# A recurrence on one Trainium2 core: 16 columns of half B's z product go ahead of A2, and the x products of a block start 17 steps ahead instead of 16

## The chip, the cores and the metric

The kernel runs on one core of one Trainium2 chip. The metric is the device time of one execution in microseconds (us). TensorE multiplies matrices (PE in the profile, its weight loads PEld), VectorE (DVE) and ScalarE (ACT) read its results from PSUM, GpSimd (POOL) works on SBUF alone, and SyncE (SP) issues the DMAs.

## The reference

A gated recurrence over 512 time steps, with a batch of 8 and 512 units, all in float32; its input is added to its output:

```python
def step(h, x_t):
    fused = sigmoid(concatenate([x_t, h], -1) @ w_W + w_b)
    hidden_state, output_state = split(fused, 2, -1)
    memory_state = x_t @ wx_W + wx_b + hidden_state * (h @ wh_W + wh_b)
    h_new = output_state * h + (1.0 - output_state) * tanh(memory_state)
    return (h_new, h_new)
_, hs = scan(step, cond_1024, swapaxes(x, 0, 1))
return x + swapaxes(hs, 0, 1)
```

In the kernel's names, r is `hidden_state` and z is `output_state`. What depends on h must be computed step by step; what depends on x alone can be computed ahead.

## The kernel before, in words

**The recurrence.** The 512 units are cut into four chunks of 128. Chunks 0 and 1 are half A, chunks 2 and 3 are half B. The state h lies in `hT` with the units of a chunk on the partitions, and a ring of eight buffers holds it, one for each of eight steps. Four steps form a group, and all products of a group go into one set of three PSUM banks: `A` (256 columns: 64 of half B's h product, then half A's h product, z and r), `D` (128 columns: half B's z, then its r) and `H` (64 columns: the rest of half B's h product). There are two sets, for groups in turn.

Each step multiplies the new state by the recurrent weights in the order of the table `ORDER`: "A0" is bank A with chunk 0, and so on. A0 and A1 are 256 columns wide, A2 and A3 are 192 (the last of bank A's columns), D0 to D3 are 128, H2 and H3 are 64. Each entry is four matmuls, one for each 32 output partitions. In the trace each matmul counts twice, with a weight load ahead of each.

VectorE and ScalarE then make the new state (`turn_r`, `turn_h`, `turn_z`, `memory`, `update`): VectorE transposes half A's columns of bank A (`tr<-A`, `md1A<-A`, `tz<-A`), ScalarE takes the sigmoids, VectorE's scan forms the argument of tanh (`m`), ScalarE takes the tanh, and another scan forms the new state of half A, chunk by chunk. Half B follows from `md1B<-A`, `tr<-D`, `sz<-D` and `md1B<-H`. A0 and A1 need half A's state alone, A2, A3 and D2, D3, H2, H3 need half B's.

**The x side.** x is cut into blocks of 16 steps. For each block, the x part of all gates is computed by a nested scheme of seven products in each of seven (`products`), 49 units of 96 columns, three units in a step and four in one step of 16 (`deal`). They run behind H in TensorE's order. GpSimd forms the sums of x that the scheme needs (`x_sum`, `inner_x`). VectorE drains finished products from PSUM (`drain`, line 429: 384 or 288 columns), DMAs on SP's queue move parts of them between partitions (lines 431 and 433, `ff<-tt` and `ff<-ff`), GpSimd adds them up (`result`, line 448), and the sums end in `xs`. From there VectorE's `turn_x` (line 317) and ScalarE's `spread` (line 312) put the x part into the next group's buffers and banks, as the table `AHEAD` says for each of the last three steps of a group. The first blocks get their x part by plain passes, dealt over the first steps (`PLAIN` lists the steps with four passes instead of three).

`LEAD` is the number of steps by which a block's products begin ahead of the block. The steps of `drain`, of GpSimd's sums and of `result` are counted from it. The order of the work on each engine is the order of this program text; nothing reorders it but TensorE, which loads weights ahead of the running matmul.

Of the kernel before, what the change touches and what calls it, by code (L numbers as in the profile page):

```python
# [23 lines left out]
LAST = 4  # L24
SYNC = mybir.DependencyInfo(mybir.DependencyClass.Sync, mybir.DependencyReason.DATA)

ORDER = "A0 A1 A2 A3 D0 D1 D2 D3 H2 H3"

FIRST = "A0 A1 x A2 x x A3 H0 H1 H2 H3 x D0 D1 D2 D3"

# [22 lines left out]

PIECE = (((0, 384), (384, 672)), ((960, 1344), (672, 960)))

LEAD = 16

AHEAD = (
    (((), ""), ((0, 1), "AD"), ((2, 3), "H")),
    (((0,), "A"), ((1, 2), "D"), ((3,), "H")),  # L60
    (((0,), "A"), ((1,), "D"), ((2, 3), "H")),
    (((0,), "A"), ((1,), "D"), ((2, 3), "H")),
)

PLAIN = (5, 10, 15)

COLS = slice(64, 448)

# [6 lines left out]
def tile_cond_rnn_residual(  # L75
# [88 lines left out]
    wd = const.tile([P, NQ, NQ, 128], F32, name="wd")  # L164
# [51 lines left out]
    def mm(out_, lhsT, rhs, start=False):  # L216
        nc.tensor.matmul(  # L217
            out_, lhsT, rhs, start=start, stop=False, skip_group_check=True
        )
# [7 lines left out]
    def bank_of(g):  # L227

        return {2: whole[1]["H"], 3: whole[1]["A"], 4: whole[1]["D"]}.get(g, xps[g % 2])
# [70 lines left out]
    def keep(g):  # L300

        nc.scalar.copy(xs[g % GS][:, SC], bank_of(g)[:, COLS])
# [5 lines left out]
    def spread(g, names):  # L308

        for n in names:  # L310
            skip = 64 if n == "A" and not g else 0
            nc.scalar.copy(banks[g % 2][n][:, skip:], source(g, XP[n].start + skip, XP[n].stop))
# [59 lines left out]
    def x_sums(c):  # L372
        jobs = [(x_sum, c, n) for n in range(4)]
        return jobs + [(inner_x, c, n, p) for n in range(4) for p in (0, 2, 3)]
# [75 lines left out]
    def take(it, n=None):  # L450
        while n is None or n > 0:
            if next(it, it) is it:
                return
            n = None if n is None else n - 1
# [5 lines left out]
    def deal(it, n):  # L460

        while n > 0 and next(it, it) is None:
            n -= it.send(n)
# [28 lines left out]
    def at_step(i, *todo):  # L492
        jobs.setdefault(i, []).extend(todo)
# [10 lines left out]
    for c in range(2, NCH):  # L504
        w0 = TC * c - LEAD
        sums = x_sums(c)
        for n, q in enumerate(sums):
            late_one = n == len(sums) - 1
            at_step(w0 - 10 + n // 2 if c == 2 else w0 if late_one else w0 - 12 + (n + 1) // 2, q)
        unit = 0  # L510
        for q, order in zip(STAGES, ORDERS):
            for name in order:
                unit += PASS[name][2] // BL
                if name in (order[1], order[3]):
                    w = min((unit - 1) // 3, TC - 1)
                    drains.setdefault(w0 + w, []).append((q, PASS[name][0]))
        for e, w, jobs_ in ((0, 12, ((0, 3), (2, 4), (1,), (5, 6))), (1, 17, ((0, 3), (1, 2), (4, 5), (6,)))):
            for m, todo in enumerate(jobs_):
                at_step(w0 + w + m, *[(result, e, n) for n in todo])

    pool_done = {}
    for i in range(T):
        g, s = divmod(i, GS)
        c, t = divmod(i, TC)
        ps = banks[g % 2]
        if c > 0 and t in (1, 4, 7, 10):
            e, k = divmod(t // 3, 2)
# [4 lines left out]
        k_ = 0  # L532
        for n in (ORDER if i else FIRST).split():
            if n == "x":
                take(first[1], 1)
                if k_ == 0:
                    keep(2)
                k_ += 1
                continue
            bank, k = n[0], int(n[1])  # L540
            hs = hT[k // 2][i % NH][:, :, k % 2, 2]
            to, w_ = {
                "A": (ps["A"], wa) if k < 2 else (ps["A"][:, 64:], wa[:, :, :, 64:]),
                "D": (ps["D"], wd),
                "H": (ps["H"], wa[:, :, :, :64]),
            }[bank]
            if bank == "A" and i == 0:
                to, w_ = xps[0][:, :HALF], wa[:, :, :, 64:]
            for j in range(NQ):
                mm(to[32 * j : 32 * j + 32, :], hs, w_[:, k, j])  # L550
        if i == 0:
            take(first[1])
        elif i <= PLAIN[-1]:
            take(first[4], 3 + (i in PLAIN))
        else:
            deal(later, 4 if (i + LEAD) % TC == TC - 1 else 3)

# [138 lines left out]
        elif i > 3 and 0 < s and g + 1 < NG:  # L696
# [1 line left out]
            for e in es:  # L698
                turn_x(g + 1, e)
            spread(g + 1, names)  # L700
        if i in PLAIN:
            keep(4 + i // 5)
        if i == 6:
            seed(7)
        for w in late.get(i, ()):
# [107 lines left out]
```

## Time and profile before

| | |
|---|---|
| Time, median of 3 runs | 1630.92 us (1630.65 to 1631.48) |
| The profiled execution, its own time | 1628.26 us |
| Its span, first to last instruction | 1626.5 us |
| Busy: PE, PEld, DVE, ACT, POOL | 1616.7, 1308.8, 1413.1, 1024.2, 541.3 us |
| Granted TensorE clock | 1.0 throughout |
| DMA | 62.04 MB, 38 GB/s over the span |

The span holds 512 steps of some 3.1 us each. A row of the timeline gives the start in us, how long the row lasts, engine, line, operation, output and inputs, shape, how many equal instructions were merged, and in brackets the idle time before it and what ended it. A row that merges several matmuls shows the shape of the first: a row of bank A with x32 holds the 256-column products and the 192-column ones. A matmul's record reaches to the modelled end of its pass through the array, so records overlap, and the busy share of PE says less than the distance from one block's start to the next one's.

### The profile page before, as it was taken

Reading aid. Unit: us, or ns where it says so; the run is one execution under the profiler, and the core shown is the slowest. Engines: PE = TensorE matmul, PEld = TensorE weight load, DVE = VectorE, ACT = ScalarE, POOL = GpSimd, SP = SyncE. Lnnn points to the kernel's source line nnn. Section 1 sums busy time; section 2 is a strip of 40 time slices with the busy share of each in tenths; the row PEclk is TensorE's granted clock in tenths of the full one; section 3 lists DMA queues with packets and bytes.
Section 4 is the critical chain, followed back from the end, with each engine's and each line's share of the span. In section 5 each row is a group of like instructions: output and inputs, shape, how many; then the busy total and the mean of one; then the engine's idle time right before and its main releaser. Section 6 shows DMA issues by size and latency. Waiting matters only on the chain.

```text
span 1626.5 us, 120027 instructions
## 1 busy us (share of the span) xinstructions
PE 1616.7 (99%) x49211; PEld 1308.8 (80%) x49211; DVE 1413.1 (87%) x11757; ACT 1024.2 (63%) x6033; POOL 541.3 (33%) x1443
## 2 busy tenths in 40 slices
PE   9999999999999999999999999999999999999998
PEld 6888888888888888888888888888888888888876
DVE  8988888888888888888888888888888888888887
ACT  4666666666666666666666666666666666666665
POOL 2323333333333333333333333333333333333321
PEclk9999999999999999999999999999999999999999
DMA  4011111111111111111111111111111111111110
GB/s 192 12 34 34 31 39 38 38 35 30 36 41 41 31 31 35 42 38 33 33 33 39 38 38 35 29 37 41 41 31 31 35 42 38 33 34 28 32 35 10
DMA packets 66217, 62.04 MB, mean 38 GB/s; under 512 B 9856, under 2 KB 64000, under 8 KB 65664
## 3 DMA queue, kind: packets, MB, share of 16 engines
q1 hardware_dynamic: 65664, 54.35, 12.7%
q8 instruction: 385, 6.31, 1.7%
q14 instruction: 168, 1.38, 0.3%
HBM read 14.96 MB, written 8.39 MB: 14 GB/s over the span
## 4 chain that ended last, share of the span: by engine, by line
PE 98%; DVE 2%; issue 0%; ACT 0%
PE A L217 49%; PE D L217 27%; PE xp L217 16%; PE H L217 7%; DVE tr L575 0%; DVE m L563 0%; DVE md1B L634 0%; DVE hT L563 0%; DVE md1A L590 0%; DVE tz L575 0%; DVE zeros L183 0%; DVE hd0B L627 0%; DVE md1B L590 0%; DVE idle L598 0%; ACT hT L283 0%
## 5 line engine op out<-in xcount | busy, mean ns | idle before, releaser
L217 PE MATMUL A<-wa,hT 128*32 128x256 f32 x16352 | 877.7, 355 | 4.3 <-DVE hT L563 4.3
L217 PEld LDWEIGHTS A<-wa,hT 128*32 128x32 f32 x16352 | 497.9, 123 | 260.9 <-DVE hT L563 135.2
L217 PE MATMUL D<-wd,hT 128*32 128x128 f32 x16384 | 541.0, 273 | 0.0
L217 PEld LDWEIGHTS D<-wd,hT 128*32 128x32 f32 x16384 | 480.6, 122 | 21.6 <-DMA wd<-in_wd_dram 0.4
L729 POOL TENSOR_TENSOR ot<-xin,hT 128x32 f32<-128x32 f32 x503 | 135.2, 269 | 1040.9 <-DVE hT L563 960.2
L283 ACT ACTIVATE md0A<-tr 128x16 f32<-128x16 f32 x512 | 112.9, 220 | 384.0 <-DVE tr L575 383.9
L283 ACT ACTIVATE hT<-m 128x8 f32<-128x8 f32 x2048 | 324.1, 207 | 48.0 <-DVE m L563 2.4
L575 DVE STREAM_TRANSPOSE tr<-A 128x64 f32<-128x64 f32 x511 | 127.7, 250 | 198.0 <-PE A L217 197.1
L283 ACT ACTIVATE hT<-hT 128x16 f32<-128x16 f32 x1024 | 232.1, 227 | 92.0 <-DVE hT L563 85.4
L217 PE MATMUL H<-wa,hT 128*32 128x64 f32 x8208 | 208.3, 219 | 0.0
L283 ACT ACTIVATE md0B<-tr 128x8 f32<-128x8 f32 x1024 | 160.0, 206 | 42.5 <-DVE tr L575 1.2
L217 PEld LDWEIGHTS H<-wa,hT 128*32 128x32 f32 x8208 | 185.8, 122 | 0.0
L563 DVE TENSOR_TENSOR_SCAN hT<-hd0B,hT 128x24 f32<-128x24 f32 x1024 | 171.7, 208 | 1.1 <-DVE hT L563 1.1
L563 DVE TENSOR_TENSOR_SCAN hT<-hd0A,hT 128x24 f32<-128x24 f32 x1024 | 172.2, 168 | 0.0
L563 DVE TENSOR_TENSOR_SCAN m<-md0B,md1B 128x24 f32<-128x24 f32 x1024 | 154.4, 192 | 0.4 <-issue 0.4
L627 DVE STREAM_TRANSPOSE hd0B<-sz 128x32 f32<-128x32 f32 x1024 | 148.6, 190 | 0.0
L563 DVE TENSOR_TENSOR_SCAN m<-md0A,md1A 128x16 f32<-128x16 f32 x1024 | 143.6, 182 | 5.5
L217 PE MATMUL xp<-ti,si 128*32 128x192 f32 (+1 forms) x3120 | 146.7, 295 | 0.0
L448 POOL TENSOR_TENSOR xs<-ff 128x192 f32<-128x192 f32 x240 | 139.8, 599 | 0.0
L634 DVE STREAM_TRANSPOSE md1B<-A 128x64 f32<-128x64 f32 x511 | 129.9, 254 | 0.0
L283 ACT ACTIVATE hd0A<-tz 128x16 f32<-128x16 f32 x512 | 116.6, 228 | 20.9
L590 DVE STREAM_TRANSPOSE md1B<-H 128x64 f32<-128x64 f32 x512 | 128.1, 250 | 0.0
(110 smaller groups left out, 1860.3 us busy)
## 6 DMA issues: line engine op xcount, KB each, us to landing
ff<-tt SPq DMA_DIRECT2D x120, 96.0 KB, 2.1
ff<-tt SPq DMA_DIRECT2D x120, 72.0 KB, 2.0
out_dram<-ot SPq DMA_DIRECT2D x128, 64.0 KB, 1.8
xin<-in_x_dram SPq DMA_DIRECT2D x112, 64.0 KB, 2.2
ff<-ff SPq DMA_DIRECT2D x60, 96.0 KB, 3.0
ff<-ff SPq DMA_DIRECT2D x60, 72.0 KB, 2.2
wx<-in_wx_dram SPq DMA_DIRECT2D x4, 768.0 KB, 7.3
wa<-in_wa_dram SPq DMA_DIRECT2D x4, 512.0 KB, 11.1
```

The source lines that it names most:

```text
L217: nc.tensor.matmul(out_, lhsT, rhs, start=start, stop=False, skip_group_check=True)
L283: inst = nc.scalar.activation(out_, in_, func, **kw).ins
L448: nc.gpsimd.tensor_tensor(to, a, b, ALU.add)
L563: return nc.vector.tensor_tensor_scan(*[t_[:, :, c_].rearrange("p n c s -> p (n c s)") for t_ in (out_, d0, d1)], 0.0, ALU.mult, ALU.add,).ins
L575: inst = nc.vector.transpose(t_.rearrange("p c n -> p (c n)"), raw[n][hf]).ins
L590: inst = nc.vector.transpose(md1[hf][g % 2][:, :, :, hf].rearrange("p n c -> p c n"), raw["h"][hf]).ins
L627: nc.vector.transpose(hd0[1][i % 2][:, :, q, 2], sz[:, 32 * q : 32 * q + 32]).ins
L634: nc.vector.transpose(md1[1][g % 2][:, :, :, 0].rearrange("p n c -> p c n"), ps["A"][:, :HU])
L729: pool_done[i + 1] = nc.gpsimd.tensor_tensor(ot[:, t], x_of(c, slice(0, NQ), t, 1), hTs[(i + 1) % NH][:, :, :, B * s1 : B * s1 + B, 2].rea ...
```

## The change

The table `ORDER` gets two new kinds of entry. "F0" is the first 16 columns (`AHEAD_D`) of bank D with chunk 0, placed between A1 and A2; "L0" is the other 112 columns, where D0 stood. `LEAD` becomes 17; the steps of GpSimd's jobs are given one more, so that they stay where they were, while the products and their drains go one step earlier. `AHEAD` deals `turn_x` and `spread` differently, and `PLAIN` and the new `DONE` deal the 48 plain passes over 14 steps instead of 15.

```diff
-ORDER = "A0 A1 A2 A3 D0 D1 D2 D3 H2 H3"
+ORDER = "A0 A1 F0 A2 A3 L0 D1 D2 D3 H2 H3"
+
+AHEAD_D = 16
...
-LEAD = 16
+LEAD = 17
 
 AHEAD = (
-    (((), ""), ((0, 1), "AD"), ((2, 3), "H")),
+    (((), ""), ((0,), "AD"), ((1, 2, 3), "H")),
+    (((0,), "A"), ((1,), "D"), ((2, 3), "H")),
+    (((0,), "A"), ((1, 2, 3), "D"), ((), "H")),
     (((0,), "A"), ((1, 2), "D"), ((3,), "H")),
-    (((0,), "A"), ((1,), "D"), ((2, 3), "H")),
-    (((0,), "A"), ((1,), "D"), ((2, 3), "H")),
 )
 
-PLAIN = (5, 10, 15)
+PLAIN = (5, 6, 7, 8, 9, 14)
+
+DONE = (5, 9, 14)
...
-            at_step(w0 - 10 + n // 2 if c == 2 else w0 if late_one else w0 - 12 + (n + 1) // 2, q)
+            at_step(w0 - 9 + n // 2 if c == 2 else w0 + 1 if late_one else w0 - 11 + (n + 1) // 2, q)
...
-        for e, w, jobs_ in ((0, 12, ((0, 3), (2, 4), (1,), (5, 6))), (1, 17, ((0, 3), (1, 2), (4, 5), (6,)))):
+        for e, w, jobs_ in ((0, 13, ((0, 3), (2, 4), (1,), (5, 6))), (1, 18, ((0, 3), (1, 2), (4, 5), (6,)))):
...
                 "D": (ps["D"], wd),
+                "F": (ps["D"][:, :AHEAD_D], wd[:, :, :, :AHEAD_D]),
+                "L": (ps["D"][:, AHEAD_D:], wd[:, :, :, AHEAD_D:]),
                 "H": (ps["H"], wa[:, :, :, :64]),
...
-        if i in PLAIN:
-            keep(4 + i // 5)
+        if i in DONE:
+            keep(5 + DONE.index(i))
```

TensorE, one step of a later block, before: the state's buffer is `hT5`, and the rows behind H are x products.

```order
L217 MATMUL A1_172<-wa_79,hT5_95 32x256 x8
L217 MATMUL A1_172<-wa_79,hT5_95 32x192 x8
L217 MATMUL D1_173<-wd_86,hT5_95 32x128 x16
L217 MATMUL H1_174<-wa_79,hT5_95 32x64 x8
L217 MATMUL xp1_176<-ti_150,si0_153 32x192 x4
L217 MATMUL xp1_176<-ti_150,si0_153 32x96 x4
```

The same step in the changed kernel:

```order
L221 MATMUL A1_172<-wa_79,hT5_95 32x256 x8
L221 MATMUL D1_173<-wd_86,hT5_95 32x16 x4
L221 MATMUL A1_172<-wa_79,hT5_95 32x192 x8
L221 MATMUL D1_173<-wd_86,hT5_95 32x112 x4
L221 MATMUL D1_173<-wd_86,hT5_95 32x128 x12
L221 MATMUL H1_174<-wa_79,hT5_95 32x64 x8
L221 MATMUL xp1_176<-ti_150,so0_151 32x192 x4
L221 MATMUL xp1_176<-ti_150,so0_151 32x96 x4
```

Four matmuls of 16 columns now stand between the 256-column and the 192-column products of bank A, the first four of D have 112 columns, and the x products behind H are those that stood one step later.

VectorE, the end of step 107 (its number stands in `m1_107` and `sz_107`), before: the drain is the row of line 429.

```order
L563 SCALAR_TENSOR_TENSOR m1_107_10358<-md0B0_100,md1B0_104 128x24 x2
L627 STREAM_TRANSPOSE hd0B1_109<-sz_107_10376 128x32 x2
L630 MEMSET idle_148 128x1
L563 SCALAR_TENSOR_TENSOR hT4_94<-hd0B1_109,hT3_93 128x24 x2
L429 TENSOR_TENSOR tt_162<-xp1_176,ee2_159 128x288
L317 STREAM_TRANSPOSE md1B1_105<-xs3_166 128x32 x2
L708 MEMSET idle_148 128x1 x2
L575 STREAM_TRANSPOSE tr0_108_10455<-A1_172 128x64
```

The end of the same step in the changed kernel, where the drain is the row of line 433:

```order
L569 SCALAR_TENSOR_TENSOR m1_107_10798<-md0B0_100,md1B0_104 128x24 x2
L633 STREAM_TRANSPOSE hd0B1_109<-sz_107_10816 128x32 x2
L636 MEMSET idle_148 128x1
L569 SCALAR_TENSOR_TENSOR hT4_94<-hd0B1_109,hT3_93 128x24 x2
L433 TENSOR_TENSOR ff1_161<-xp0_175,ee1_158 128x384
L321 STREAM_TRANSPOSE md1B1_105<-xs3_166 128x32
L714 MEMSET idle_148 128x1 x2
L581 STREAM_TRANSPOSE tr0_108_10897<-A1_172 128x64
```

The drain into `tt`, whose DMAs GpSimd's jobs of step 108 read, stood at the end of step 107 and stands one step earlier now; the drain that stood in step 108 takes its place, and of the two transposes of `xs` one remains here. GpSimd's rows are the same in both kernels, in the same order.

## The prediction

> **What bounds the kernel now.** I read the page's busy shares and chain first, then the timeline of one step in the middle, then a step near the end that has no x products, then the single blocks of TensorE.
>
> ```profile
> PE 1616.7 (99%) x49211; PEld 1308.8 (80%) x49211; DVE 1413.1 (87%) x11757; ACT 1024.2 (63%) x6033; POOL 541.3 (33%) x1443
> ...
> PE 98%; DVE 2%; issue 0%; ACT 0%
> ```
>
> Read alone, this says that TensorE sets the time and that any column moved into an idle moment is a gain. The step shows something else. These are TensorE's products in two steps of the middle, and then its weight loads:
>
> ```profile
> 800.76 1.71 PE L217 MATMUL A<-wa,hT 128*32 128x256 f32 x32
> 802.29 1.06 PE L217 MATMUL D<-wd,hT 128*32 128x128 f32 x32
> 803.16 0.41 PE L217 MATMUL H<-wa,hT 128*32 128x64 f32 x16
> 803.39 0.35 PE L217 MATMUL xp<-wx,so 128*32 128x96 f32 x8
> 803.55 0.51 PE L217 MATMUL xp<-ti,si 128*32 128x192 f32 x8
> 803.88 1.72 PE L217 MATMUL A<-wa,hT 128*32 128x256 f32 x32
> 805.41 1.06 PE L217 MATMUL D<-wd,hT 128*32 128x128 f32 x32
> ```
>
> ```profile
> 803.81 0.64 PEld L217 LDWEIGHTS A<-wa,hT 128*32 128x32 f32 x16
> 804.72 0.51 PEld L217 LDWEIGHTS A<-wa,hT 128*32 128x32 f32 x16 [0.26 <-DVE hT L563]
> 805.25 0.96 PEld L217 LDWEIGHTS D<-wd,hT 128*32 128x32 f32 x32
> ```
>
> A step takes 3.12 us (800.76 to 803.88). Each chunk of h makes two blocks in the trace, and a block is four products that start together, one for each 32 output partitions. So D is 8 blocks of 128 columns in 0.87 us (802.29 to 803.16), 0.109 each, and H is 4 blocks of 64 columns in 0.23, 0.057 each: some 0.82 ns a column. By that rate a block of 256 columns takes 0.216 and one of 192 takes 0.162, and the step's products add up to 4 x 0.216 + 4 x 0.162 + 0.87 + 0.23 + 0.49 (xp, 803.39 to 803.88) = 3.10 us. TensorE is nearly full, but 0.02 us is missing. It is lost ahead of A2: the loads for A2 wait for half B's state until 804.72, as the row says.
>
> Whether TensorE or the recurrence sets 3.12 us is told by the last steps, where no x products are left. Loads first, then products:
>
> ```profile
> 1601.11 0.61 PEld L217 LDWEIGHTS A<-wa,hT 128*32 128x32 f32 x16 [0.39 <-DVE hT L563]
> 1602.01 0.51 PEld L217 LDWEIGHTS A<-wa,hT 128*32 128x32 f32 x16 [0.29 <-DVE hT L563]
> ...
> 1604.22 0.62 PEld L217 LDWEIGHTS A<-wa,hT 128*32 128x32 f32 x16 [0.39 <-DVE hT L563]
> ```
>
> ```profile
> 1601.11 1.78 PE L217 MATMUL A<-wa,hT 128*32 128x256 f32 x32 [0.24 <-DVE hT L563]
> 1602.70 1.06 PE L217 MATMUL D<-wd,hT 128*32 128x128 f32 x32
> ```
>
> There TensorE has 0.49 us less to do and idles, and the step still takes 3.11 us (1601.11 to 1604.22). So the loop sets the time: half B's state, A2 and A3, the transposes and scans on VectorE, the new state. VectorE releases half A's state and half B's 0.90 to 0.91 us apart in both places (1601.11 and 1602.01; 803.81 and 804.72), and A0 and A1 must fit between them.
>
> **The change part by part.** *The 16 columns.* Four matmuls are added to each of 511 steps (the first step has its own order), which is two blocks of 16 columns between A1 and A2; D's first two blocks shrink to 112 columns. What is given back, 2 x 16 x 0.82 ns = 0.027 us, lies behind A3, outside the loop, and only adds to TensorE's slack: I count nothing for it, and where TensorE itself is the bound I subtract it. What can be hidden is the room ahead of A2. For it I need the time from a load that was waited for to its product; the rows are a place where A0's loads came late, the first block's and the second block's, then the duration of that first block's products, the loads', and the usual one:
>
> ```profile
> 365.40 0.14 PEld L217 LDWEIGHTS A<-wa,hT 128*32 128x32 f32 x4 [0.44 <-DVE hT L563]
> ...
> 365.44 0.15 PEld L217 LDWEIGHTS A<-wa,hT 128*32 128x32 f32 x4
> ```
>
> ```profile
> L217 PEld LDWEIGHTS A<-wa,hT x8: 121/127/134, 365.4 to 365.5; 128*32 128x32 f32 x8
> L217 PE MATMUL A<-wa,hT x4: 418/418/418, 365.4 to 365.4; 128*32 128x256 f32 x4
> ...
> L217 PE MATMUL A<-wa,hT 128*32 128x256 f32 x4912 | 321.3, 379 | 0.0
> ```
>
> A product whose load has just been issued is recorded 418 ns long where 379 is usual, so it begins about 0.04 us after its load, and the next block's loads go out 0.03 to 0.04 us after the first block's. The room follows. In the middle step A0 could begin at 803.81 + 0.04 = 803.85, and TensorE reaches it at 803.88; A1 ends at 803.88 + 4 x 0.216 = 804.74, and A2 begins at 804.72 + 0.04 = 804.76. The room is 0.03 + 0.02. In the late step A1 ends at 1601.11 + 0.04 + 0.864 = 1602.014 and A2 begins at 1602.05: 0.036. I take 0.04 us.
>
> What the two blocks occupy is not in the trace, where no block is narrower than H's 64 columns. Bound from below by the rate: H's 0.057 less 48 columns of 0.82 ns is 0.018, twice 0.036. Bound from above by the loads: a block's weights are loaded while the block ahead of it runs, one block ahead and no further (D's first loads go out at 805.25 and D starts at 805.41, 0.16 later, which is A3's last block), and a 16-column block is over before the next load is done. The first block's weights are there in time, under A1's last block. The second block's loads go out when the first block starts; A2's loads can go out only when the second block has taken its weights, 0.035 later (the spacing of the two load rows), and A2 begins 0.04 after that: 0.075 us, and at most 2 x 0.04 = 0.08 if the loads do not overlap at all. I take 0.075, because a run of loads that nothing hides is just what the rows at 365.40 show. That is 0.035 more than the room. Nothing hides it: A2 is late by 0.035, so is everything on VectorE behind it, and half A's state of the next step with it. 511 x 0.035 = 17.9 us. The new blocks wait besides for ScalarE's read of D (sz) of the step before, done long since, so I count nothing for that wait.
>
> In one step of each chunk four units of x products are dealt instead of three, and there TensorE is the bound. The row before and after such a step:
>
> ```profile
> 871.24 0.25 DVE L575 STREAM_TRANSPOSE tr<-A 128x64 f32<-128x64 f32 x1 [0.26 <-PE A L217]
> ...
> 874.50 0.25 DVE L575 STREAM_TRANSPOSE tr<-A 128x64 f32<-128x64 f32 x1 [0.30 <-PE A L217]
> ```
>
> It takes 3.26 us. There the blocks cost 0.075 - 0.027 = 0.048, which is 0.013 over what I counted: 30 x 0.013 = 0.4 us.
>
> *Seventeen steps ahead.* The sums of the x products (drains, VectorE) and the DMAs behind them go one step earlier; GpSimd's jobs stay in their absolute steps, so a DMA has a step more to land. This is what a late one costs. The rows are GpSimd's and VectorE's at such a place, VectorE's scans in an ordinary step, and the waits:
>
> ```profile
> 364.10 1.18 POOL L448 TENSOR_TENSOR ff<-ff 128x192 f32<-128x192 f32 x2 [0.95 <-DMA ff<-tt]
> ...
> 364.20 0.64 DVE L563 TENSOR_TENSOR_SCAN m<-md0A,md1A 128x16 f32<-128x16 f32 x2
> ...
> 803.08 0.28 DVE L563 TENSOR_TENSOR_SCAN m<-md0A,md1A 128x16 f32<-128x16 f32 x2
> ```
>
> ```profile
> POOL ot L729 <- DMA ff<-ff: 5.6, 3, 2.1
> POOL ff L448 <- DMA ff<-tt: 4.3, 7, 1.2
> ```
>
> GpSimd's sum, released late, runs beside the scans of the loop, and they take 0.64 instead of 0.28 us. There are 10 such waits, each of at most 2.1 us and so shorter than the step that is won. Between nothing and 10 x 0.36 I take 0.2 each, since a wait may end clear of the scans: 2.0 us gained. On SP's queue a drain's DMA now passes one load of x or one store, each under a step long; nobody is close to those. VectorE's drains and turn_x are dealt so that no step gets more than a wide drain with one transpose or a narrow one with two, which is no more than before; the 0.40 us that VectorE waits for A in an ordinary step (802.54, below) stays its cover. At the start six steps instead of three have a fourth pass, for the same 48 passes: between 0 and 3 x 0.14 us, I take 0.2.
>
> *Sum.* 17.9 + 0.4 - 2.0 + 0.2 = 16.5 us. The profiled execution took 1628.26 (its span 1626.5 and 1.8 around it), so 1644.8; the median of the three timed runs is 2.66 above it, so the forecast is 1647 us, slower by 1.0%.
>
> **Rivals.** *Hidden.* If a 16-column block costs only its columns, the two fill 0.036 us of a room of 0.04, and the loop keeps its length. What is left is the gain at the DMAs: 1630.9 - 2.0 + 0.2 = 1629 us. For it speaks that the H blocks, half as wide as D's, show no cost beyond their columns; against it that H's 0.057 still covers a load of 0.04, and 0.018 does not. It decides below 0.04 us for the pair.
>
> *Issue alone.* Four loads last 0.14 us together and 0.121 each, so they go out 0.0065 apart, 0.027 for four. If loads pipeline and only that issue is left, the pair takes 0.054 and overruns by 0.014: 511 x 0.014 = 7.2, less 1.8, 1636 us. Against it speaks the spacing of 0.03 to 0.04 between the two load rows, where nothing but loads went on.
>
> The Trainium skill, "TensorE: Matmul & The Clock Gate", section "LDWEIGHTS (loading the stationary operand)", puts a load at its columns over 1.2 GHz, an estimate of 27 ns for 32 columns. By that page the result would be this rival's; no run here has shown such a block yet, and the load rows are nearer to 35 ns.
>
> *D is the real limit.* VectorE's transposes of A and of D, against the ends of those products (800.76 + 1.71 = 802.47; 802.29 + 1.06 = 803.35):
>
> ```profile
> 802.54 0.25 DVE L575 STREAM_TRANSPOSE tr<-A 128x64 f32<-128x64 f32 x1 [0.40 <-PE A L217]
> ...
> 803.27 0.25 DVE L634 STREAM_TRANSPOSE md1B<-A 128x64 f32<-128x64 f32 x1
> 803.42 0.24 DVE L575 STREAM_TRANSPOSE tr<-D 128x64 f32<-128x64 f32 x1
> ```
>
> ```profile
> 363.41 1.06 PE L217 MATMUL D<-wd,hT 128*32 128x128 f32 x32
> ...
> 364.77 0.24 DVE L634 STREAM_TRANSPOSE md1B<-A 128x64 f32<-128x64 f32 x1
> 364.92 0.20 DVE L575 STREAM_TRANSPOSE tr<-D 128x64 f32<-128x64 f32 x1
> ```
>
> Both transposes start 0.07 us after the end of what they read, and tr<-A certainly waited. If D is late too, taking 0.027 us out of it shortens every step: with the blocks hidden, 1629 - 511 x 0.027 = 1615 us. Against it: 0.15 us lie between md1B and tr<-D there, and just as many where D had been done for 0.45 us (364.47 against 364.92). VectorE's own pace sets that start.
>
> **How the numbers follow.** Forecast 0.62, hidden 0.18, issue alone 0.13, D 0.05, something else 0.02. The forecast's own range is 1642 to 1650, from 0.065 to 0.08 us for the pair; a miss of the DMA gain lies within it at 1649. The whole range reaches down to the hidden case and takes in issue alone: 1628 to 1653. A measurement can tell about 0.2%, 3.3 us, from no change. Slower by more: the forecast and nearly all of issue alone, 0.75. Within: most of the hidden case, 0.18. Faster by more: D and the best of the hidden case, 0.07.
>
> **What would show it.** In the new trace the loads for A2 should follow the first 16-column block by some 0.035 us instead of waiting for half B's state; A2's first product should begin about 0.98 us after A0's loads, where it is 0.95 now (803.81 to 804.76); a step should last 3.15 to 3.16 us with x products, and nearly as long without them at the end, against 3.11. Ordinary A-to-A steps of 3.12 would mean that the blocks are hidden, and shorter ones that D was the limit. GpSimd should have no wait for DMA ff<-tt, and no scan pair of 0.64. The forecast is wrong if the array takes the weights of two 16-column blocks faster than those of a 256-column block that was waited for.

## The result and the profile after

| | us |
|---|---|
| Before, median of 4 runs | 1630.79 (1630.04 to 1631.48) |
| Changed kernel, median of 4 runs | 1656.32 (1654.83 to 1656.79) |
| Ratio, 95% interval | 1.0156 [1.0144, 1.0168] |
| Profiled execution of the changed kernel, its span | 1654.83, 1652.7 |

The change costs 25.5 us, 1.6%. The direction was the forecast one, and so was the mechanism, but the time lies 9.3 us above the forecast and 3.3 us above the range. The granted clock is 0.999 or 1.0 in every run.

The changed kernel's page, busy shares and the chain of waits:

```profile
PE 1642.5 (99%) x53299; PEld 1405.9 (85%) x53299; DVE 1412.4 (85%) x11757; ACT 1023.3 (62%) x6033; POOL 538.1 (33%) x1443
...
PE 98%; DVE 1%; issue 0%; ACT 0%
```

It reads almost as before: the busy shares don't tell what has happened. The step does. First TensorE's products in one step of the middle (start, duration, and so on, as before), then the weight loads of the same step:

```profile
803.75 1.05 PE L221 MATMUL A<-wa,hT 128*32 128x256 f32 x16
804.62 0.24 PE L221 MATMUL D<-wd,hT 128*32 128x16 f32 x8
804.69 0.85 PE L221 MATMUL A<-wa,hT 128*32 128x192 f32 x16
805.36 1.03 PE L221 MATMUL D<-wd,hT 128*32 128x112 f32 x32
806.21 0.40 PE L221 MATMUL H<-wa,hT 128*32 128x64 f32 x16
806.92 0.40 PE L221 MATMUL A<-wa,hT 128*32 128x256 f32 x4
```

```profile
803.71 0.61 PEld L221 LDWEIGHTS A<-wa,hT 128*32 128x32 f32 x16
804.41 0.35 PEld L221 LDWEIGHTS D<-wd,hT 128*32 128x32 f32 x8
804.66 0.52 PEld L221 LDWEIGHTS A<-wa,hT 128*32 128x32 f32 x16
```

The step lasts 3.17 us (803.75 to 806.92), where it was 3.12. A2's loads at 804.66 no longer carry a wait for half B's state: they stand behind the two narrow blocks. The table of waits says the same for the whole run (engine, tile and line, what it waited for, us in total, times, the longest):

```profile
PEld A L221 <- DVE hT L569: 22.0, 109, 0.5
```

In the kernel before, that group held 135.2 us in 500 waits, 481 of them A2's. Only four of A2's are left; the other 105 are waits of A0's loads.

How long the pair takes is read at the end of A1. First the products and loads of the window around it, grouped by shape with the mean duration in ns behind the total, then the start of the second narrow block's loads:

```profile
L221 PE MATMUL A<-wa,hT 128*32 128x192 f32 x2 | 0.3, 344 | 0.0
L221 PE MATMUL D<-wd,hT 128*32 128x16 f32 x8 | 0.2, 186 | 0.0
L221 PEld LDWEIGHTS A<-wa,hT 128*32 128x32 f32 x4 | 0.1, 133 | 0.0
L221 PEld LDWEIGHTS D<-wd,hT 128*32 128x32 f32 x4 | 0.1, 122 | 0.1
```

```profile
804.62 0.14 PEld L221 LDWEIGHTS D<-wd,hT 128*32 128x32 f32 x4
```

A1 ends at 803.75 + 4 x 0.216 = 804.62; there the first narrow block starts and the second one's loads go out. A2's loads follow at 804.66, directly behind these, and they are recorded 133 ns long where a load usually takes 122. A2's first product is recorded from 804.69 with 344 ns, where a product of 192 columns that waits for no load has 326 (xp in the same kernel), so by the reading that the prediction used it begins 0.02 later, at 804.71. The pair takes 0.09 us, 0.045 a block; over all steps the median from A1's end to A2's first product is 0.090.

Steps without x products, near the end; A0's loads, A2's, and A0's of the next step:

```profile
1630.08 0.62 PEld L221 LDWEIGHTS A<-wa,hT 128*32 128x32 f32 x16 [0.41 <-DVE hT L569]
1631.02 0.52 PEld L221 LDWEIGHTS A<-wa,hT 128*32 128x32 f32 x16
...
1633.24 0.62 PEld L221 LDWEIGHTS A<-wa,hT 128*32 128x32 f32 x16 [0.42 <-DVE hT L569]
```

The step there lasts 3.16 us with 0.49 us less for TensorE to do, and only A0's loads still wait for a state. So the length of the step is the loop's.

**Where 26.2 us of span came from.** I take the distance from one `tr<-A` to the next as a step. From step 16 on its median is 3.166 us, before 3.116: 495 x 0.050 = 24.75 us. The 30 steps with four units are 0.157 above their median instead of 0.144, with their neighbours 0.5 us in all. The steps that a late DMA made long are gone, 2.2 us; some other irregular ones add 0.4. Steps 1 to 15 take 49.5 us instead of 47.7, 1.8 more, of which 15 x 0.05 is the same cost; and the first `tr<-A` comes at 25.2 us instead of 24.4. Sum: 24.75 + 0.5 - (2.2 - 0.4) + 1.8 + 0.9 = 26.2.

### The profile page after: what moved, and what is told of

Its sections match the earlier page's. It is cut to its first block, busy times and chain, and to the rows that moved or that the text cites. A ratio compares the mean times of both kernels' runs of the same rounds, so it can differ in the third digit from the quotient of the medians.

```text
span 1652.7 us, 128203 instructions
## 1 busy us (share of the span) xinstructions
PE 1642.5 (99%) x53299; PEld 1405.9 (85%) x53299; DVE 1412.4 (85%) x11757; ACT 1023.3 (62%) x6033; POOL 538.1 (33%) x1443
## 4 chain that ended last, share of the span: by engine, by line
PE 98%; DVE 1%; issue 0%; ACT 0%
PE A L221 48%; PE D L221 28%; PE xp L221 16%; PE H L221 7%; DVE tr L581 0%; DVE m L569 0%; DVE hT L569 0%; DVE md1B L640 0%; DVE md1A L596 0%; DVE tz L581 0%; DVE zeros L187 0%; DVE hd0B L633 0%; DVE md1B L596 0%; DVE idle L604 0%; ACT hT L287 0%
## 5 line engine op out<-in xcount | busy, mean ns | idle before, releaser
L221 PE MATMUL A<-wa,hT 128*32 128x256 f32 x16352 | 918.4, 355 | 4.5 <-DVE hT L569 4.5
L221 PEld LDWEIGHTS D<-wd,hT 128*32 128x32 f32 x20472 | 620.8, 122 | 89.5 <-issue 0.3
L221 PE MATMUL D<-wd,hT 128*32 128x112 f32 (+1 forms) x20472 | 656.4, 253 | 0.0
L221 PEld LDWEIGHTS A<-wa,hT 128*32 128x32 f32 x16352 | 503.8, 125 | 123.2 <-DVE hT L569 22.0
L569 DVE TENSOR_TENSOR_SCAN hT<-hd0A,hT 128x24 f32<-128x24 f32 x1024 | 184.6, 180 | 0.0
```

The lines of the kernel that those rows point to most:

```text
L221: nc.tensor.matmul(out_, lhsT, rhs, start=start, stop=False, skip_group_check=True)
L569: return nc.vector.tensor_tensor_scan(*[t_[:, :, c_].rearrange("p n c s -> p (n c s)") for t_ in (out_, d0, d1)], 0.0, ALU.mult, ALU.add,).ins
```

## The experiments

Each kernel was timed beside the kernel before on the same chip, whose medians there lay between 1630.1 and 1630.9 us; the ratios are to these. 64 columns, twice 8 columns and 16 columns behind A3 have two executions each, the others four to eleven. "Step" is the median distance between successive `tr<-A` from step 16 on, "tail" that of the last 15 or 16 steps, which have no x products; A1 to A2 is the median from the end of A1's last block to A2's first product.

| kernel | us | ratio, 95% | step | tail | A1 to A2 |
|---|---|---|---|---|---|
| before | 1630.8 | | 3.116 | 3.109 | |
| changed | 1656.3 | 1.0156 [1.0144, 1.0168] | 3.166 | 3.165 | 0.090 |
| 16 columns alone | 1661.7 | 1.0187 [1.0172, 1.0203] | 3.167 | 3.163 | 0.090 |
| 17 steps alone | 1628.6 | 0.9987 [0.9978, 0.9995] | 3.119 | 3.112 | |
| D 16 columns shorter | 1629.0 | 0.9988 [0.9979, 0.9997] | 3.117 | 3.110 | |
| 32 columns ahead | 1653.9 | 1.0142 [1.0128, 1.0156] | 3.167 | 3.164 | 0.090 |
| 64 columns ahead | 1662.1 | 1.0195 [1.0165, 1.0225] | 3.187 | 3.186 | 0.111 |
| twice 8 columns ahead | 1714.3 | 1.0516 [1.0456, 1.0575] | 3.259 | 3.257 | 0.182 |
| 16 columns behind A3 | 1660.8 | 1.0187 [1.0158, 1.0217] | 3.179 | 3.167 | |
| one block of zeros | 1641.7 | 1.0071 [1.0054, 1.0088] | 3.143 | 3.118 | 0.042 |
| two blocks of zeros | 1656.4 | 1.0160 [1.0145, 1.0175] | 3.171 | 3.147 | 0.070 |

### The 16 columns alone

```diff
-ORDER = "A0 A1 A2 A3 D0 D1 D2 D3 H2 H3"
+ORDER = "A0 A1 F0 A2 A3 L0 D1 D2 D3 H2 H3"
+
+AHEAD_D = 16
...
```

This is the kernel before with the new entries of `ORDER` and 16 steps of lead; the dots stand for the two rows that say what "F" and "L" are.

> The 16 columns alone, on the kernel before, with its 16 steps. Load chain (two narrow blocks take 0.09 us in a room of 0.04, because A2's load can go out only behind the second block): steps of 3.166 us as in the changed kernel, 511 x 0.05 = +25.5 us, and the waits of GpSimd for DMAs stay: 1656 to 1658 us. Rival, the 17 steps carry a part of the loss: clearly less than that, 1650 us or below.

Measured: 1661.7, some 4 us above the expectation. The step is that of the changed kernel, 3.167, so the whole lengthening belongs to the 16 columns. The rest lies at the DMAs. The waits of this kernel's GpSimd:

```profile
POOL ff L450 <- DMA ff<-tt: 13.8, 23, 1.3
...
POOL ot L733 <- DMA ff<-ff: 1.6, 1, 1.6
```

There are 24 waits for these DMAs instead of the 11 of the kernel before (the prediction's ten, and one of 2.4 us of `ot` for `ff<-tt` that it left out), and the steps at that place of the block are 6.4 us longer than the median in sum instead of 2.2. Why they became more was not tried.

### The seventeen steps alone

```diff
-ORDER = "A0 A1 F0 A2 A3 L0 D1 D2 D3 H2 H3"
+ORDER = "A0 A1 A2 A3 D0 D1 D2 D3 H2 H3"
```

This is the changed kernel with the old `ORDER`.

> The 17 steps alone, with the order of the kernel before on TensorE. Load chain: steps of 3.116 us, the long steps with late DMAs are gone (-2 us), the first 15 steps cost up to 1 us: 1629 to 1631 us. Rival, the 17 steps carry a part of the loss: 1635 us or more.

Measured: 1628.6, 2.35 us below the kernel before on that chip (1630.91), and the interval excludes one. GpSimd has no wait for `ff<-tt` or `ff<-ff` left, and steps 1 to 15 take 47.9 us, 0.2 more than before. The ordinary step is 0.003 us longer than before, which nothing here explains. This version is the fastest of the three, by 0.13% of the kernel before. On top of the 16 columns the seventeen steps are worth 1661.7 - 1656.3 = 5.4 us, since there the long steps that they remove come to 6.4 us; so the two parts do not simply add (30.75 - 2.35 = 28.4, measured 25.5).

### D 16 columns shorter

```diff
-ORDER = "A0 A1 A2 A3 D0 D1 D2 D3 H2 H3"
+ORDER = "A0 A1 A2 A3 L0 D1 D2 D3 H2 H3"
...
```

The kernel before, with 16 columns of half B's z product with chunk 0 left out altogether.

> The kernel before with D's first block pair cut to 112 columns and nothing put in front; 16 columns of half B's z product with chunk 0 are left out, so TensorE has 0.027 us less to do in every step. The loop as the limit: 1630 to 1631 us, no change, steps of 3.116. Rival, D or TensorE's sum is the limit: up to 511 x 0.027 = 13.8 us faster, 1617 us.

Measured: 1629.0, 1.96 us below the kernel before on that chip and a little below the expectation; the step stays at 3.117. Loads of A0 in two steps of the middle:

```profile
904.59 0.62 PEld L219 LDWEIGHTS A<-wa,hT 128*32 128x32 f32 x16 [0.15 <-DVE hT L567]
...
907.70 0.62 PEld L219 LDWEIGHTS A<-wa,hT 128*32 128x32 f32 x16
```

3.11 us, though TensorE has less to do: D is not what the loop waits for, and what is taken from it gains nothing in an ordinary step. Of the little that is gained, 0.8 us lies in the steps with four units, where TensorE is the bound: they are 0.116 above the median instead of 0.144, and 30 x 0.028 = 0.8. Where the rest comes from was not found.

### 32 and 64 columns ahead

```diff
-AHEAD_D = 16
+AHEAD_D = 32
```

and likewise with 64, in the changed kernel.

> The changed kernel with 32 columns ahead instead of 16. Load chain: a 32-column block runs 0.028 us, still less than the 0.04 that a load takes, so the pair takes the same 0.09: 1655 to 1657 us, steps of 3.166. Rival, the cost is columns: 32 columns more in the loop, +0.026 us a step, 1669 us.

> The changed kernel with 64 columns ahead. Load chain: a 64-column block runs 0.055 us and covers the next load (0.04 to 0.053), so columns set the pair now, 0.11 us: steps of 3.116 + 0.11 - 0.04 = 3.186, +0.02 against the changed kernel, 1666 to 1668 us. Rival, every column costs beside a fixed part (0.09 for 16): 0.09 + 96 x 0.82 ns = 0.17, steps of 3.245, 1696 us.

Measured: with 32 columns the step is the same as with 16, 3.167. The time is 1653.9, 1.1 us below the expectation and 2.4 below the changed kernel, which the two intervals do not separate. The four-unit steps are shorter (0.130 above the median, not 0.157), because TensorE gets 16 more columns back behind A3 for the same price ahead of A2; that is 30 x 0.027 = 0.8 us of it. With 64 the step is 3.187, as expected, but the time, 1662.1, is 4 us below the expectation: that had not counted the four-unit steps, which are only 0.078 above the median there, 30 x 0.079 = 2.4 us less than in the changed kernel. The products of both kernels around the pair, 32 columns first:

```profile
906.45 0.26 PE L221 MATMUL D<-wd,hT 128*32 128x32 f32 x8
906.52 0.86 PE L221 MATMUL A<-wa,hT 128*32 128x192 f32 x16
```

```profile
903.95 0.29 PE L221 MATMUL D<-wd,hT 128*32 128x64 f32 x8
904.06 0.83 PE L221 MATMUL A<-wa,hT 128*32 128x192 f32 x16
```

From the first narrow record to A2's record it is 0.07 us for 32 columns, as for 16 (804.62 to 804.69), and 0.11 for 64. So a float32 block of 16 or 32 columns costs about 0.045 us, until its columns take longer: a block of 64 takes 0.055. By 0.82 to 0.85 ns a column (the prediction's rate, and D's 0.109 us for 128) the two meet at some 54 columns, an estimate.

### Twice 8 columns

```diff
-ORDER = "A0 A1 F0 A2 A3 L0 D1 D2 D3 H2 H3"
+ORDER = "A0 A1 F0 G0 A2 A3 L0 D1 D2 D3 H2 H3"
...
```

"F0" and "G0" are now 8 columns each: the same columns ahead of A2, in four blocks.

> The changed kernel with the 16 columns as two products of 8 instead of one: as many columns, four blocks instead of two. Load chain: each further block takes 0.036 to 0.047 us, so the four take 0.16 to 0.185 and a step 3.24 to 3.26: 1693 to 1704 us. Rival, the cost is columns: no change, 1656 us.

Measured: the step is 3.259, at the upper end of the expectation; the four blocks take 0.182 us, again 0.045 each. The price goes by the number of blocks, not by columns. The two executions lie 8 us apart (1710.2 and 1718.4), and their median is 10 us above the expectation: in the profiled one, irregular long steps add 21.5 us to the median ones. A part of that is idle time of TensorE that ends with nothing that the profile shows, named "issue". The waits of that name from 25 us on:

```profile
PEld D L221 <- issue: 4.9, 16, 0.6
PEld xp L221 <- issue: 3.4, 11, 0.6
PEld A L221 <- issue: 0.8, 5, 0.2
PEld H L221 <- issue: 0.6, 2, 0.4
```

These are 9.7 us in 34 places, three of them ahead of step 16 (1.1 us). The kernel before has 0.3 us in one such place, the changed one 0.9 in four; the first 25 us, which are setup, hold 7.4 to 10.7 us of the same name in every kernel.

The traces show more than the name says. The places lie a multiple of 256 TensorE instructions apart (products and loads counted, give or take one), all 34 here and all four in the changed kernel. The page's DMA queue of the kind "instruction" moves 16,384 bytes at a time, and it does so once for 256 TensorE instructions: 385 times for the 98,422 of the kernel before, 448 times for the 114,774 of this one:

```profile
q8 instruction: 448, 7.34, 1.8%
```

So TensorE stops at one place in a block of 256 of its own instructions. Most blocks pass without a stop; why some do not was not tried, and the rest of the 21.5 us was not traced.

### The 16 columns behind A3

```diff
-ORDER = "A0 A1 F0 A2 A3 L0 D1 D2 D3 H2 H3"
+ORDER = "A0 A1 A2 A3 F0 L0 D1 D2 D3 H2 H3"
```

The same blocks, outside the stretch that the prediction named.

> The changed kernel with F0 behind A3, right ahead of L0, instead of ahead of A2; the same instructions. Load chain: the pair still takes 0.09 us where its columns were worth 0.027, outside the gap, so TensorE's own sum is 3.10 + 0.063 = 3.163 and sets the steps with x products, 1650 to 1656 us, while the last 15 steps, which have none, go back to 3.11. Rival, the loss comes only from lying between A1 and A2: 1630 us.

Measured: 1660.8, 5 us above the expectation. With x products the step is 3.179: TensorE's own 3.163, and 0.016 by which A2 begins late behind A1 because its loads wait for half B's state, as in the kernel before. The tail missed the expectation: the step stays at 3.167 where no x products are left. TensorE is not the bound there, as A0's loads in the tail of this kernel show:

```profile
1621.34 0.62 PEld L221 LDWEIGHTS A<-wa,hT 128*32 128x32 f32 x16 [0.39 <-DVE hT L569]
1622.23 0.51 PEld L221 LDWEIGHTS A<-wa,hT 128*32 128x32 f32 x16 [0.28 <-DVE hT L569]
1624.51 0.61 PEld L221 LDWEIGHTS A<-wa,hT 128*32 128x32 f32 x16 [0.39 <-DVE hT L569]
```

Both halves are waited for again, and the states themselves come later. VectorE's rows in a step of the middle say why:

```profile
904.86 0.26 DVE L640 STREAM_TRANSPOSE md1B<-A 128x64 f32<-128x64 f32 x1
905.06 0.25 DVE L581 STREAM_TRANSPOSE tr<-D 128x64 f32<-128x64 f32 x1
905.24 0.17 DVE L569 TENSOR_TENSOR_SCAN hT<-hd0A,hT 128x24 f32<-128x24 f32 x1
```

`tr<-D` stands 0.20 us behind `md1B<-A`, not 0.15 as in the kernel before; over all steps the medians are 0.208 and 0.151, and it starts 67 ns after D's last product, while before it started 76 ns after it. So D had only 0.009 us of slack. The two narrow blocks end D later by 2 x (0.045 - 0.013) = 0.064, and all but the slack of that, some 0.055, enters the loop by another door: 3.109 + 0.055 = 3.164. In the tail the blocks cost about as much on either side of A2 and A3, 0.058 us behind and 0.056 ahead.

### Blocks of zeros

```diff
-ORDER = "A0 A1 F0 A2 A3 L0 D1 D2 D3 H2 H3"
+ORDER = "A0 A1 z A2 A3 D0 D1 D2 D3 H2 H3"
...
+            if n == "z":
+                for j in range(NQ):
+                    mm(ps["D"][32 * j : 32 * j + 32, :AHEAD_D], none[:, :32], none[:, :AHEAD_D])
+                continue
```

A z is one block of 16 columns in bf16 that adds zeros; D keeps its full width, and the lead is 17. The second kernel has "A0 A1 z z A2".

> The 17 steps alone, and between A1 and A2 one block of four bf16 products of 16 columns with zeros, which adds nothing to D; bf16 makes one block where float32 makes two. Load chain: one block takes about 0.045 us, which is the room of 0.04, so steps grow by 0 to 0.01 us against the 17 steps alone (1628.6): 1628 to 1634 us. Rival, any product between A1 and A2 disturbs the loop, whatever its length: steps of 3.166, 1654 us.

> The same with two such blocks of zeros in every step. Load chain: two blocks take 0.09 us as the two float32 blocks do, steps of 3.16 to 3.17 and 1651 to 1656 us, though D keeps its whole width and no product of D is moved. Rival, the loss comes from moving D's columns (its reads, its banks): as with one block, 1634 us or less.

One block missed the expectation in the steps with x products, 3.143 instead of 3.12 to 3.13, and so in the time, 1641.7 instead of 1628 to 1634. In the tail it was as expected, 3.118 against 3.112 for the seventeen steps alone. The loads of two steps with x products, and of a step in the tail:

```profile
904.36 0.67 PEld L221 LDWEIGHTS A<-wa,hT 128*32 128x32 f32 x16
...
907.51 0.67 PEld L221 LDWEIGHTS A<-wa,hT 128*32 128x32 f32 x16
```

```profile
1601.42 0.61 PEld L221 LDWEIGHTS A<-wa,hT 128*32 128x32 f32 x16 [0.39 <-DVE hT L573]
1602.11 0.12 PEld L221 LDWEIGHTS <-none 128*32 128x32 bf16 x4
1602.32 0.51 PEld L221 LDWEIGHTS A<-wa,hT 128*32 128x32 f32 x16
...
1604.54 0.62 PEld L221 LDWEIGHTS A<-wa,hT 128*32 128x32 f32 x16 [0.39 <-DVE hT L573]
```

In the tail one block of 0.042 us fits into the room ahead of A2 and the loop hardly feels it: the room of 0.04 is confirmed. In the middle the loads of A0 wait for nothing: there TensorE's own 3.10 plus 0.042 is longer than the loop, because nothing was taken from D in return.

Two blocks, loads of A0, of the zeros and of A2 in the tail, and A0's of the next step:

```profile
1619.02 0.62 PEld L221 LDWEIGHTS A<-wa,hT 128*32 128x32 f32 x16 [0.39 <-DVE hT L573]
1619.71 0.34 PEld L221 LDWEIGHTS <-none 128*32 128x32 bf16 x8
1619.95 0.51 PEld L221 LDWEIGHTS A<-wa,hT 128*32 128x32 f32 x16
...
1622.16 0.62 PEld L221 LDWEIGHTS A<-wa,hT 128*32 128x32 f32 x16 [0.39 <-DVE hT L573]
```

They lengthen the tail by 0.035 (3.147 against 3.112), while not a column of D was moved: the price is that of the blocks' presence ahead of A2. But they take 0.070 us, not the 0.09 of the expectation. That the time, 1656.4, still came out at the upper end of the expected range is luck: the middle step of 3.171 is TensorE's own 3.10 + 0.070, not the loop. The second of these blocks adds only 0.028 us, with as many loads and products as a float32 block of 0.045, so the number of instructions does not set the 0.045.

## Why the prediction came out as it did

**What bounds the kernel.** Right. The loop sets the step: the tail of the changed kernel is as long as its middle, and with D 16 columns shorter the step did not change. That last run also removes the rival "D is the real limit" as it was put; but D has only 0.009 us to spare, as the run with the blocks behind A3 showed, so the sentence "VectorE's own pace sets that start" is true by a hair. The prediction had not found this. Its widths of 0.216 and 0.162 us for blocks of 256 and 192 columns are those of the trace, but they follow from 0.844 ns a column and not from its 0.82.

**The room ahead of A2, 0.04 us.** Right: one block of 0.042 costs 0.006 in the tail.

**The pair, 0.075 us.** This is the step that failed. Its last part read: "A2's loads can go out only when the second block has taken its weights, 0.035 later (the spacing of the two load rows), and A2 begins 0.04 after that". The first part measured 0.036 (loads at 804.62 and 804.66). The second measured 0.053, not 0.04: the 0.04 was read off a load that found the loads' path empty, A0's at 365.40, while A2's loads stand directly behind others. The row that tells it was in the prediction, "121/127/134": the loads of the block behind were recorded up to 134 ns long, those ahead 121. What makes the last part longer is not shown: with the two blocks of zeros A2's loads go out just as closely behind others, and A2 begins 0.041 after them. The bound from above, 2 x 0.04, was made of the same short value and so was no bound. With 0.090 the overrun is 0.050 instead of 0.035, and 511 x 0.050 = 25.6 in place of 17.9: 7.7 us, of the 9.3 by which the time lies above the forecast. Most of the rest lies in the first 75 us ("Prologue", below).

The page rule beside the rival "issue alone" belongs here. The Trainium skill, "TensorE: Matmul & The Clock Gate", section "LDWEIGHTS (loading the stationary operand)", puts a load at its columns over 1.2 GHz, an estimate of 27 ns for 32 columns. A float32 block with such loads costs more in these traces, 0.045 us at 8, 16 and 32 columns; only the second block of bf16 zeros, 0.028, is near it.

**Four-unit steps, 0.4 us.** Measured 0.5. TensorE's own sum is now 3.10 - 0.027 + 0.09 = 3.163, as long as the loop's 3.166, so both limits meet.

**Seventeen steps, a gain of 2.0 us.** Right for the part alone: 2.35 in time, and no GpSimd wait for `ff<-tt` and no long steps from it in the changed kernel. The prediction counted ten waits of at most 2.1 us; there are eleven, of at most 2.4.

**Prologue, 0.2 us.** Right for the deal of the passes alone (47.9 against 47.7). In the changed kernel steps 1 to 15 take a further 0.9 us beyond the price of the pair, and the first step comes 0.9 us later. TensorE stops there where nothing is named. Its loads, the first row during the setup, the others in the early steps:

```profile
7.06 0.16 PEld L221 LDWEIGHTS xp<-wx,head 128*32 128x32 f32 x8 [1.27 <-issue]
...
58.72 0.23 PEld L221 LDWEIGHTS H<-wa,hT 128*32 128x32 f32 x11 [0.24 <-issue]
...
62.45 0.40 PEld L221 LDWEIGHTS xp<-wx,xin 128*32 128x32 f32 x19 [0.28 <-issue]
...
66.18 0.12 PEld L221 LDWEIGHTS xp<-wx,xin 128*32 128x32 f32 x3 [0.24 <-issue]
```

In the kernel before, the load of the first row went out at 6.00, and from 55 to 68 us it has no such wait. The last three stops are 256 TensorE instructions apart, as in the run with twice 8 columns. Every kernel that moves columns of D into blocks of their own begins late, by 0.9 to 2.1 us, the one with the blocks behind A3 as well. The number of TensorE's instructions alone does not explain it: the kernel with two blocks of zeros has as many as the changed one (53,299 products) and begins 0.25 us late. The cause stays open.

**Hidden and issue alone.** Refuted: the one needed a pair of less than 0.04 us, the other one of 0.054, and it takes 0.090. Only a single block comes near to hidden.

**What would show it.** A2's loads follow the first narrow block by 0.036, as said; A2's first product begins 0.995 us after A0's loads (median; 0.98 was said); the step lasts 3.166 (3.15 to 3.16 was said).

## What to carry to other kernels

A small piece of work that is moved into an idle moment of TensorE costs what its blocks cost, not what its columns cost: here 0.045 us for every block of four narrow float32 products, so if anything is moved, move few and wide blocks, and compare the block's price with the idle moment, not with the engine's busy share. Take the delay from a load to its product from a row where the load stands behind other loads, if it will stand so; a load that found the engine idle gave too small a number here (0.041 for 0.053 us), and no upper bound. When a chain has two inputs that end within 0.01 us of each other, a cost moved from one to the other stays a cost.

## What the runs showed of the hardware

- A block of four products (32-column loads, float32), with others ahead of A2, takes about 0.045 us at 8, 16 and 32 columns, and 0.055 at 64, where its columns decide. Blocks of bf16 zeros, whose loads are recorded 97 ns long instead of 122, take 0.042 for one and 0.070 for two.
- A2's first product begins 0.041 us after its loads where these waited for a state, and 0.053 us after them where they stand directly behind the loads of a narrow float32 block; behind those of a narrow bf16 block it is again 0.041.
- TensorE's stops that the profile names "issue" lie, from 25 us on, a multiple of 256 TensorE instructions apart (34 of 34 with twice 8 columns, four of four in the changed kernel), and the queue "instruction" makes one transfer of 16,384 bytes for 256 of them (448 for 114,774).
- Where D ends earlier, `tr<-D` is recorded 0.22 us long instead of 0.24 (rows of the changed kernel; the run with D 16 columns shorter shows the same 0.22):

```profile
803.17 0.25 DVE L640 STREAM_TRANSPOSE md1B<-A 128x64 f32<-128x64 f32 x1
803.32 0.22 DVE L581 STREAM_TRANSPOSE tr<-D 128x64 f32<-128x64 f32 x1
803.46 0.20 DVE L569 TENSOR_TENSOR_SCAN hT<-hd0A,hT 128x24 f32<-128x24 f32 x1
803.58 0.25 DVE L596 STREAM_TRANSPOSE md1B<-H 128x64 f32<-128x64 f32 x1
```

  The scan behind it starts earlier, but lasts 0.20 instead of 0.17, and `md1B<-H` starts the same 0.25 us after `tr<-D` as before. So these records on VectorE start earlier and end no earlier.
